# Self-attention of a Perceiver block: VectorE's sum of squares moved between the halves of the scores, the output scaled before the row sums, two copies of values moved from ScalarE

## The chip, the core and the metric

The kernel runs on one core of a Trainium2 chip. The core has five engines that run side by side, each with its own queue of instructions that it takes in order: TensorE (PE in the profile; its weight loads are the row PEld), VectorE (DVE), ScalarE (ACT), GpSimd (POOL) and SyncE (SP), which here only issues DMAs. An instruction that needs the result of another engine waits for a semaphore, and everything behind it on its own engine waits too. The metric is the time of one execution on the device in microseconds, less being better.

## What is computed

A block of three layers over x, 16 sequences of 64 latents with 512 features, each layer adding to x: a cross attention to a context of 512 tokens for each sequence, a differential self attention among the 64 latents, and a feed-forward network whose inputs and weights are rounded to FP4 blocks of 16. Each layer starts with a layer norm without weights. The change touches only the self attention:

```
q, k = rope(x @ Wq.T), rope(x @ Wk.T)        # 8 heads, each of two halves of 32
v    = x @ Wv.T                              # 8 heads of 64
w1   = softmax(q1 @ k1.T * 32**-0.25)
w2   = softmax(q2 @ k2.T * 32**-0.25)
o    = (w1 - lam * w2) @ v
ms   = mean(o * o, axis=-1)                  # for each row and head
o    = (o * rsqrt(ms + eps) * ln_w + ln_b) * (1 - LAMBDA_INIT)
x    = x + o @ Wo.T
```

## The kernel before, in words

The 1024 rows of x are eight tiles x0 to x7 of 128 rows, two sequences each. Products with weights run as three matmul groups: data and weights are split into a high and a low part, and high x high, high x low and low x high are added in PSUM (`terms`, L121, three groups of four matmuls for a 128x512 output).

The program has four parts: the preparation of the latents, the cross attention over 16 sequences (with the quantising of the feed-forward weights in between), the self attention, and the feed-forward network. Self attention overlaps with its neighbours: tiles 0 and 1 are started inside the last part of the cross attention (end of `cross_attention`), tiles 2 to 7 are the loop of `SelfAttention.rest`, and the last steps of tiles 6 and 7 lie among the first matmuls of the feed-forward network.

The steps for one tile t, and their engines, are:

- `product` (PE, L121): Wq, Wk and Wv of the tile; `rope` (DVE L1218 and L1220, then an addition on POOL, L1226) makes rc_q and rc_k.
- `values` (ACT, L1201): four copies of 64x256 that take the values out of PSUM, two (h) for each sequence e of the tile.
- `turn_qk` (PE L171, ACT L1236): transposes qt and kt, copied to qT and kT; `turn` does the same for the next tile's normalised input (zt, then zh on ACT and zl on DVE, L129 and L130); `turn_w` for the attention weights (wt, wT).
- `scores` (PE L1248): 64 small matmuls into two PSUM tiles, sc_0 and sc_1, one for each half of the heads' pairs.
- `softmax` (DVE): for each half a maximum (L1265, mx) and a subtraction (L1266, ex). `exp` (ACT L1275) then takes both halves in one instruction.
- `sum` (DVE L1280 to L1283): the row sums, their reciprocal, and the factor of lambda. `mix` multiplies by them (DVE L1288) and adds the two softmaxes on POOL (L1291, tile w).
- `weigh` (PE L1316): attention weights times values, output o in two PSUM tiles. `squares` (ACT L1327) squares it into SBUF, `rms` sums the squares (DVE L1332, ms) and has POOL make the reciprocal root (`rstd`: L136, then a power at L137). `scale` (DVE L1338, two instructions) multiplies o by it.
- `turn_o` (PE L171, tile ot): transposes the scaled output; ACT applies ln_w and ln_b (L1348) and makes the high part (L129), POOL the low part (L130, ol). `out` (PE): the product with Wo, tile wo; DVE adds it to x (L1368).

In one pass n of the loop these steps belong to three tiles: the products of tile n, the mixing of tile n-1 and the output of tile n-2; `end(n)` at the close of the pass holds the scores and softmax of tile n together with weigh, squares and rms of tile n-1. `end` is also called for tiles 0 and 1.

The order on each engine is the order in which the program records its instructions, fixed by `in_order`, which ties each instruction of an engine to the one before it. Some preparing steps of the feed-forward network are placed among them. DVE's order for tile n within `end` and the next pass is: mx, ex (first half), mx, ex (second half), ms of tile n-1, the row sums of tile n, and then, in the next pass, `scale` of tile n-1, `mix` of tile n, `rope` of tile n+1. POOL's order is: the power for tile n-1, w of tile n, ol of tile n-1, rc_q and rc_k of tile n+1. On PE the transposes ot of tile n-1 stand between Wk and Wv of tile n+1.

PSUM has three tiles of one bank for products and transposes (`ps_mm`), which are handed round: a matmul that writes one waits until the last reader of its previous content is done.

Of the kernel before, what the change touches and what calls it, by code (L numbers as in the profile page):

```python
# [9 lines left out]
F32 = mybir.dt.float32  # L10
# [9 lines left out]
P = 128  # L20
# [3 lines left out]
S = 64  # L24
N = 512
NJ = N // P
NT = B * S // P
# [427 lines left out]
def _latents(ctx, tc, cm, sc, i, cw, cx, sa):  # L455
# [261 lines left out]
    for g, _ in enumerate(groups):  # L717
        heads(g, "k", w_k, sc.k, 1.0)
        heads(g, "q", w_q, sc.q, S**-0.5, cw.bq)
        if g + 1 < len(groups):  # L720
            for p in groups[g + 1]:
                turn(p)
                upper(p)
                lower(p)
        values(g)
# [3 lines left out]
def cross_attention(tc, cm, sc, i, cw, cx, w1, w2, att, quant):  # L729
# [263 lines left out]
    for b in range(B):  # L993
# [38 lines left out]
        if last:  # L1032
            att.split("Wq", 2)
        scores(b, 0)
        softmax(b, 0)
        around(b + 1, 2, 3)
        keys(b, 3)
        cx.fetch(b + 2, 1)
        cx.low(b + 1, 2)
        cx.high(b + 1, 3)  # L1040
        tick()
        values(b, 0)
        cx.every(b + 1)
        cx.low(b + 1, 3)
# [5 lines left out]
        if b == 0:  # L1050
            load_o(0)
            load_o(1)
        values(b, 1)
        begin(b + 1)
        cx.fetch(b + 2, 2)
# [6 lines left out]
        turn(b, 0, 1)  # L1062
        scores(b, 1)
        softmax(b, 1)
        around(b + 2, 0, 1)
        if done is not None:
# [67 lines left out]
class SelfAttention:  # L1134
# [60 lines left out]
    def values(self, t):  # L1195

        v = self.st["v", t] = self.w1.tile([P, 2, KC, S], F32, tag="v", bufs=4, name=f"v_{t}")
        ps = self.st.pop(("ps", t, "Wv")).rearrange("p (c h d) -> p c h d", h=2, d=S)
        for e in range(2):
            for h in range(2):  # L1200
                self.nc.scalar.copy(v[h * S : (h + 1) * S, e], ps[e * S : (e + 1) * S, :, h, :])  # L1201

    def rope(self, t, name):
        nc, w1, sa = self.nc, self.w1, self.sa
# [48 lines left out]
                        stop=True,  # L1253
                    )

    def softmax(self, t):

        nc = self.nc
        mx = self.cm.small.tile([P, 16], F32, tag="mx", name=f"mx_{t}")
        ex = self.st["ex", t] = self.w1.tile([P, 16, S], F32, tag="q_hl", name=f"ex_{t}")  # L1260
        for n, ps in enumerate(self.st.pop(("sc", t))):
            half = slice(8 * n, 8 * n + 8)
            sc = ps[:, :, : KC * S].rearrange("p s (c t) -> p s c t", t=S)
            m = mx[:, half].rearrange("p (s c) -> p s c", s=2)
            nc.vector.tensor_reduce(m, sc, AX.X, ALU.max)  # L1265
            nc.vector.tensor_tensor(  # L1266
                ex[:, half, :].rearrange("p (s c) t -> p s c t", s=2),
                sc,
                m.unsqueeze(3).to_broadcast([P, 2, KC, S]),
                ALU.subtract,  # L1270
            )
# [97 lines left out]

    def end(self, n, sum=True):  # L1370

        if n < NT:
            self.turn_qk(n)
        if 0 <= n - 1:
            self.turn_w(n - 1)
        if n + 1 < NT:
            self.turn(n + 1)
        if n < NT:
            self.scores(n)
        if 0 <= n - 1:  # L1380
            self.weigh(n - 1)
            self.squares(n - 1)
        if n < NT:
            self.softmax(n)
            self.exp(n)
        if 0 <= n - 1:
            self.rms(n - 1)
        if n < NT and sum:
            self.sum(n)

    def rest(self, ff, last):

        first, second = (ff.norm_steps(t) for t in range(2))
        norms = iter(first[:2] + second[:1] + first[2:4] + second[1:2] + first[4:] + second[2:])


        parts = {3: (1, 0, 1), 4: (1, 2, 1), 5: (1, 2, 0), 6: (0, 2, 0), 7: (1, 2, 0)}  # L1400

        def steps(n, part):
            for _ in range(parts[n][part] if n in parts else 0):
                next(norms)()

        for n in range(2, NT):
            self.product(n, "Wq")
            self.scale(n - 2)
            self.product(n, "Wk")
            if n == NT - 1:  # L1410
                ff.weights(("g", 1))
            self.mix(n - 1)
            self.turn_o(n - 2)
            self.rope(n, "Wq")
            self.product(n, "Wv")
            if n == NT - 1:
                ff.weights(("u", 1), ("d", 0))
            self.values(n)
            if n + 1 < NT:
                self.norm(n + 1)  # L1420
            self.rope(n, "Wk")
            steps(n, 0)
            if n == NT - 1:
                ff.turn(0)
            self.out(n - 2)
            last.get(n, lambda: None)()
            if n == 2:
                ff.weights(("g", 0), ("u", 0))
            steps(n, 1)
            self.end(n)  # L1430
            steps(n, 2)
        assert not list(norms)
        ff.gate((0, 0))
        self.scale(NT - 2)
        self.mix(NT - 1)
        ff.up((0, 0))
        ff.gated((0, 0))
        self.turn_o(NT - 2)
        ff.turn(1)
        ff.gate((0, 1))  # L1440
        self.turn_w(NT - 1)
        ff.quantise((0, 0))
        ff.weights(("d", 1))
        ff.gate((1, 0))
        self.weigh(NT - 1)
        self.squares(NT - 1)
        self.rms(NT - 1)
        self.out(NT - 2)
        ff.weights(("g", 2))
        ff.up((0, 1))  # L1450
        self.scale(NT - 1)
        ff.hidden((0, 1))
        self.turn_o(NT - 1)
        ff.up((1, 0))
        ff.hidden((1, 0))
        ff.turn_h((0, 0))
        self.out(NT - 1)
        ff.weights(("u", 2), ("d", 2))
        self.cm.in_order()
# [271 lines left out]
```

## Time and profile before

| what | value |
|---|---|
| runs | 911.80, 912.67 and 987.52 us, median 912.67 us |
| the profiled execution | 912.59 us, span of the core 910.7 us |
| busy DVE, ACT, POOL in the span | 682.1, 399.9, 330.5 us |
| TensorE clock granted | 1.0 |
| from 576 to 731 us: tiles 0 to 7 of the self attention | 155 us, of which PE is busy 147.06 |
| before 576 us and after 731 us | PE busy 564.58 of 576.0, and 175.26 of 180.0 |

The profile is of one execution of 912.59 us; the span from its first to its last instruction is 1.9 us shorter. Two of the three runs and the profiled execution lie within 0.9 us of each other. A line of the timeline gives start, duration, engine, line of the code, operation, output and inputs with their sizes, the number of instructions merged, and in brackets the idle time of the engine just before, with the instruction that ended it. In what follows a time "at 645.06" is counted from the start of the span.

### The profile page before, as it was taken

To read this page: it belongs to the slowest core of one execution; us is meant where nothing else is said; L and a number is where in the kernel's file an instruction comes from. 1 tells how busy PE (TensorE), PEld (TensorE's weight loads), DVE (VectorE), ACT (ScalarE), POOL (GpSimd) and SP (SyncE) were. 2 spreads that over 40 slices of the span, in tenths; PEclk is the share of its full clock that TensorE was granted. 3 is DMA by queue.
4 is the path that set the end of the run, shared out by engine and by line. 5 is a ranking of instruction groups with operands and counts; after the bars stand their busy time and mean duration, and the time that the engine had idled before them with its cause. 6 is when DMAs were issued, how large, how long until landed. Compare 5 with 4: busy or idle time off the path is not lost.

```text
span 910.7 us, 17129 instructions
## 1 busy us (share of the span) xinstructions
PE 886.9 (97%) x6550; PEld 733.2 (81%) x6550; DVE 682.1 (75%) x1394; ACT 399.9 (44%) x782; POOL 330.5 (36%) x376
## 2 busy tenths in 40 slices
PE   5999999999999999999999999999999999999998
PEld 5898777878787887888778877778777788888886
DVE  7545467878799787786997964586878797888875
ACT  4464344544545444445444545545454423322221
POOL 5255153326254353263443621547564330100000
PEclk9999999999999999999999999999999999999999
DMA  7464565554555445345544452140005530000000
GB/s 241 176 242 138 152 187 166 152 178 146 150 161 150 159 157 174 112 138 151 161 147 144 133 149 102 47 185 2 2 1 212 229 139 12 12 12 12 13 13 24
DMA packets 80235, 111.11 MB, mean 122 GB/s; under 512 B 33161, under 2 KB 38809, under 8 KB 78873
## 3 DMA queue, kind: packets, MB, share of 16 engines
q1 hardware_dynamic: 79992, 109.48, 37.5%
q8 instruction: 52, 0.85, 0.4%
q0 software_dynamic: 160, 0.52, 0.2%
q14 instruction: 31, 0.25, 0.1%
HBM read 84.26 MB, written 25.72 MB: 121 GB/s over the span
## 4 chain that ended last, share of the span: by engine, by line
PE 85%; DVE 7%; ACT 3%; DMA 2%; issue 1%; SPq 1%; POOL 1%; ACTq 0%; DVEq 0%; POOLq 0%
PE pk L121 18%; PE pv L121 18%; PE gu L121 13%; PE dn L121 7%; PE av L904 4%; PE sim L836 4%; PE prt L171 3%; PE po L121 3%; PE Wv L121 2%; PE lv L121 2%; PE wo L121 2%; PE lq L121 2%; PE lk L121 2%; DVE ex L1266 1%; PE ht L171 1%; DMA raw_wo<-in_w_out_dram 1%
## 5 line engine op out<-in xcount | busy, mean ns | idle before, releaser
L121 PE MATMUL pv<-xvh,x 128*128 128x512 f32 x512 | 133.1, 392 | 0.0
L121 PE MATMUL pk<-x,xkh 128*128 128x512 f32 x512 | 130.5, 397 | 0.3 <-DVE k L810 0.3
L121 PEld LDWEIGHTS pk<-x,xkh 128*128 128x128 f32 x512 | 93.7, 188 | 26.0 <-issue 4.0
L121 PEld LDWEIGHTS pv<-xvh,x 128*128 128x128 f32 x512 | 95.3, 188 | 23.3 <-issue 2.2
L810 DVE TENSOR_TENSOR k<-pk,row 128x512 f32<-128x512 f32 x64 | 43.6, 683 | 47.0 <-PE pk L121 46.8
L823 ACT ACTIVATE v<-pv,rs 128x512 f32<-128x512 f32 x64 | 43.9, 686 | 79.4 <-PE pv L121 79.3
L859 ACT ACTIVATE pr<-pr,least 128x576 f32<-128x576 f32 x64 | 49.2, 772 | 55.1 <-DVE least L855 54.8
L368 POOL TENSOR_TENSOR x<-raw,x 128x512 fp32r<-128x512 f32 x32 | 44.2, 1382 | 78.0 <-ACT x L362 71.6
L121 PE MATMUL pk<-x,xkl 128*128 128x512 f32 x256 | 68.7, 390 | 0.0
L121 PE MATMUL pv<-xvl,x 128*128 128x512 f32 x256 | 68.5, 389 | 0.0
L121 PE MATMUL gu<-uT,fx 128*128 128x512 f32 (+1 forms) x288 | 67.8, 378 | 0.0
L121 PE MATMUL gu<-gT,fx 128*128 128x512 f32 (+1 forms) x288 | 65.5, 375 | 0.0
L121 PEld LDWEIGHTS gu<-gT,fx 128*128 128x128 f32 x288 | 52.3, 188 | 7.6
L121 PEld LDWEIGHTS gu<-uT,fx 128*128 128x128 f32 x288 | 51.9, 188 | 7.2
L121 PEld LDWEIGHTS pk<-x,xkl 128*128 128x128 f32 x256 | 48.1, 188 | 10.4
L121 PEld LDWEIGHTS pv<-xvl,x 128*128 128x128 f32 x256 | 48.1, 188 | 10.2
L855 DVE CUSTOM_DVE_ANT_0 pr<-sim,mask 128x576 f32<-128x576 f32 x64 | 45.9, 754 | 6.2 <-PE sim L836 5.3
L321 DVE BATCH_NORM_STATS2 cst<-nat 128x6 f32<-128x512 f32 x64 | 42.8, 669 | 3.6 <-DMA nat<-in_ctx_dram 3.6
L121 PE MATMUL dn<-dT,hh 128*128 128x512 f32 x176 | 44.7, 393 | 0.6 <-ACT hh L129 0.6
L205 ACT ACTIVATE qe_h<-qe_h,mmagic 128x512 f32<-128x512 f32 (+1 forms) x24 | 16.5, 687 | 64.3 <-DVE qe_h L202 64.3
L871 ACT COPY prT<-prt 128x512 f32<-128x512 f32 x64 | 34.1, 585 | 18.1 <-PE prt L171 18.1
L904 PEld LDWEIGHTS av<-v,prT 128*64 128x64 f32 x1024 | 36.7, 138 | 5.6 <-issue 5.6
(302 smaller groups left out, 1963.0 us busy)
## 6 DMA issues: line engine op xcount, KB each, us to landing
nat<-in_ctx_dram SPq DMA_DIRECT2D x16, 1024.0 KB
raw<-in_ctxT_dram SPq DMA_DIRECT2D x64, 256.0 KB
d_d<-qhl_d SPq DMA_DIRECT2D x11, 512.0 KB
row<-rs_d SPq DMA_DIRECT2D x16, 256.0 KB
g_d<-qhl_g SPq DMA_DIRECT2D x8, 512.0 KB
u_d<-qhl_u SPq DMA_DIRECT2D x8, 512.0 KB
gT<-g_d SPq DMA_DIRECT2D x4, 1024.0 KB
uT<-u_d SPq DMA_DIRECT2D x4, 1024.0 KB
```

What stands on the lines that cost most here:

```text
L121: self.nc.tensor.matmul(ps, lhsT=p[i], rhs=p[j], start=start and n == 0, stop=stop and n == last)
L171: self.nc.tensor.transpose(pt[:, c * P : (c + 1) * P], src[:, c * P : (c + 1) * P], self.ident)
L205: nc.scalar.activation(e, e, AF.Relu, bias=self.mmagic, scale=MAGIC)
L321: nc.vector.bn_stats(st, self.nat[b][:, j, :])
L368: by.tensor_tensor(lo, self.raw[:, c, :], f32(hi), ALU.subtract)
L810: nc.vector.tensor_tensor(k[:, S : S + N], ps, cx.row[b], ALU.mult)
L823: nc.scalar.mul(v, ps, cx.rs[b][:, t : t + 1])
L836: nc.tensor.matmul(pss[r][c * S : (c + 1) * S, h, :half], lhsT=queries[b % 2][rows, m, :], rhs=st["k"][m][rows, at : at + half], start=Tru ...
L855: nc.vector.tensor_tensor_reduce(two(pr), ps[:, :, :half], two(mask), -1.0, BIG, ALU.add, ALU.min, least)
L859: nc.scalar.activation(pr, pr, AF.Exp, bias=least, scale=-1.0, accum_out=st["tot"][:, t : t + 1])
L871: nc.scalar.copy(prT, pt.rearrange("p (j q) -> p j q", q=P))
L904: nc.tensor.matmul(st["av"][rows, 2 * a + r, :], lhsT=w[:, rows], rhs=v[:, at : at + S], start=(n == 0), stop=(n == len(pairs) - 1),)
```

## The change

Three things move; no arithmetic of the result is changed.

1. `softmax` takes the halves that it is to do, so that `end` can call it once for each half. `rms` of the tile before (the sum of squares on DVE and the two POOL instructions behind it) now stands between the halves.
2. `scale` of the tile before moves from the next pass, after the product Wq, into `end`: after `exp` and ahead of `sum`.
3. In `values`, for tile 0 alone, the two copies of the second sequence go to DVE.

```
     def values(self, t):
 ...
         for e in range(2):
+            copy = self.nc.vector.tensor_copy if t == 0 and e else self.nc.scalar.copy
             for h in range(2):
-                self.nc.scalar.copy(v[h * S : (h + 1) * S, e], ps[e * S : (e + 1) * S, :, h, :])
+                copy(v[h * S : (h + 1) * S, e], ps[e * S : (e + 1) * S, :, h, :])

-    def softmax(self, t):
+    def softmax(self, t, ns=range(2)):
 ...
     def end(self, n, sum=True):
-        if n < NT:
-            self.turn_qk(n)
-        if 0 <= n - 1:
+        self.turn_qk(n)
+        if n:
             self.turn_w(n - 1)
         if n + 1 < NT:
             self.turn(n + 1)
-        if n < NT:
-            self.scores(n)
-        if 0 <= n - 1:
+        self.scores(n)
+        if n:
             self.weigh(n - 1)
             self.squares(n - 1)
-        if n < NT:
-            self.softmax(n)
-            self.exp(n)
-        if 0 <= n - 1:
+        self.softmax(n, range(1))
+        if n:
             self.rms(n - 1)
-        if n < NT and sum:
+        self.softmax(n, range(1, 2))
+        self.exp(n)
+        if n:
+            self.scale(n - 1)
+        if sum:
             self.sum(n)

     def rest(self, ff, last):
 ...
             self.product(n, "Wq")
-            self.scale(n - 2)
             self.product(n, "Wk")
 ...
         ff.gate((0, 0))
-        self.scale(NT - 2)
         self.mix(NT - 1)
```

DVE's order becomes: mx, ex of the first half of tile n, ms of tile n-1, mx, ex of the second half, the two instructions of `scale` for tile n-1, the row sums of tile n, `mix` of tile n, `rope` of tile n+1. DVE has two instructions more and ACT two fewer, all for tile 0. The orders of PE, POOL and SP do not change. On ACT one step of the feed-forward network (the normalising fz of its tile 2, L166, in the pass of tile 7) comes two instructions later. In the changed program the two copies on DVE wait for the two on ACT, and the transposes zt of tile 1 take the PSUM tile of qt and wait for the copy qT, where they took that of the values before and waited for the four copies; the product Wq of tile 1 now takes the values' tile and waits for DVE's copies.

More of the change, by code (lines that the diff above doesn't have):

```diff
@@ L1254, in scores @@
                     )
-    def softmax(self, t):
+    def softmax(self, t, ns=range(2)):
         nc = self.nc
-        mx = self.cm.small.tile([P, 16], F32, tag="mx", name=f"mx_{t}")
-        ex = self.st["ex", t] = self.w1.tile([P, 16, S], F32, tag="q_hl", name=f"ex_{t}")
-        for n, ps in enumerate(self.st.pop(("sc", t))):
+        if ns[0] == 0:
+            self.st["mx", t] = self.cm.small.tile([P, 16], F32, tag="mx", name=f"mx_{t}")
+            self.st["ex", t] = self.w1.tile([P, 16, S], F32, tag="q_hl", name=f"ex_{t}")
+        mx, ex = self.st["mx", t], self.st["ex", t]
+        for n in ns:
+            ps = self.st["sc", t][n]
             half = slice(8 * n, 8 * n + 8)
```

## The prediction

> **What bounds the kernel now.** First the page's list of engines: TensorE is busy nearly throughout, so only a time in which it stands still can be won, and its clock is granted in full.
>
> ```profile
> PE 886.9 (97%) x6550; PEld 733.2 (81%) x6550; DVE 682.1 (75%) x1394; ACT 399.9 (44%) x782; POOL 330.5 (36%) x376
> ```
>
> Then TensorE's waits from 575 to 760 us, each row a waiting operation, its releaser, us in total, times and the longest:
>
> ```profile
> PE ot L171 <- DVE on L1338: 6.1, 7, 1.5
> PE zt L171 <- ACT v L1201: 0.8, 1, 0.8
> ```
>
> These two are what the change aims at: seven waits of the output's transposes for the scaling, and the wait for the copies of values. The first row counts from the modelled end of the matmul before. By starts it is more: a group of four matmuls follows the next at 0.91 us, so ot could start 0.91 after the last group of Wk. It starts 1.63 late for tile 0, 0.90, 0.89, 0.90, 0.87 and 0.90 for tiles 1 to 5, and 1.17 for tile 6: 7.26 us.
>
> Whether it can be won shows in the timeline of one pass, TensorE first (ot of tile 2, then the transposes of tile 4):
>
> ```profile
> 643.26 1.07 PE L121 MATMUL Wk<-Wkh,zl 128*128 128x512 f32 x4
> 645.06 0.65 PE L171 MATMUL ot<-ident,on 128*128 128x128 f32 x4 [0.73 <-DVE on L1338]
> 651.45 0.60 PE L171 MATMUL kt<-ident,rc_k 128*128 128x128 f32 x4
> ```
>
> VectorE in the same pass:
>
> ```profile
> 638.59 0.68 DVE L1265 TENSOR_REDUCE mx<-sc 128x8 f32<-128x512 f32 x1
> 639.38 0.69 DVE L1266 TENSOR_TENSOR ex<-sc,mx 128x512 f32<-128x512 f32 x1
> ...
> 641.31 0.67 DVE L1332 TENSOR_REDUCE ms<-on 128x8 f32<-128x512 f32 x1
> 642.57 1.22 DVE L1280 TENSOR_REDUCE sm<-ex 128x16 f32<-128x1024 f32 x1 [0.59 <-ACT ex L1275]
> ...
> 644.25 0.75 DVE L1338 TENSOR_TENSOR on<-o,rstd_o 128x256 f32<-128x256 f32 x2
> 644.92 1.21 DVE L1288 TENSOR_TENSOR ex<-ex,sm 128x1024 f32<-128x1024 f32 x1
> ```
>
> And GpSimd:
>
> ```profile
> 642.34 1.66 POOL L137 TENSOR_TENSOR rstd_o<-rstd_o,mhalf 128x8 f32<-128x8 f32 x1
> 646.28 1.31 POOL L1291 TENSOR_TENSOR w<-ex 128x512 f32<-128x512 f32 x1 [2.28 <-DVE ex L1288]
> 647.54 1.30 POOL L130 TENSOR_TENSOR ol<-oT,oh 128x512 fp32r<-128x512 f32 x1
> 648.80 1.29 POOL L1226 TENSOR_TENSOR rc_q<-rc_q,rs_q 128x512 f32<-128x512 f32 x1
> 650.05 1.28 POOL L1226 TENSOR_TENSOR rc_k<-rc_k,rs_k 128x512 f32<-128x512 f32 x1
> ```
>
> The reader is to see a second chain. GpSimd does w as soon as mix (644.92) is over, then ol, rc_q and rc_k without a gap, and rc_k ends at 651.33; TensorE's kt, which needs it, starts at 651.45. One pass later kt does wait, in the weight loads:
>
> ```profile
> 667.33 0.42 PEld L171 LDWEIGHTS kt<-ident,rc_k 128*128 128x128 f32 x4 [0.18 <-POOL rc_k L1226]
> ```
>
> There rc_k ended at 667.27, so kt follows it by 0.06, and the slack at 651.45 was 0.06 us. From kt it goes on to the copies, the scores, mx 2.89 later, mix, GpSimd and the next kt: a loop of 2.89 + 6.33 + 1.36 + 3.77 + 1.28 + 0.06 = 15.69 us (kt to mx, mx to mix, mix to w, w to rc_k, its length, the release) beside a pass of 15.75. **The loop over GpSimd is as long as the pass with its stall.** A stall taken from ot must come back at kt unless mix comes earlier.
>
> **The change, part by part: the pass.** I count from mx of the first half (before, 638.59 = 0). Before: ex 0.79, mx 1.39, ex 2.11, ms 2.72, exp on ScalarE 2.89 (641.48), row sums 3.98, scale 5.66, mix 6.33.
>
> After: ex 0.79, ms 1.39. Its squares are there: ScalarE ended them at 639.36 = 0.77. The second mx is 0.61 later, 2.00; its ex 0.72 on, 2.72; exp 0.78 on, 3.50; the sums could start 1.09 after that, 4.59. GpSimd starts 0.75 after ms, as before (641.31, 642.06), at 2.14; the power starts 0.28 later and takes 1.65, until 4.07; VectorE, idle from 3.41, scales at 4.12. Behind this new wait stand the row sums, mix and rope. Scaling takes 0.67 to its successor, so the sums start at 4.79, not 4.59; then 1.26 to the reciprocal, 0.29 to the lambda factor, 0.26 to mix: **mix at 6.60, which is 0.27 later than before**. The scaled output is 1.54 earlier: ot could start at 4.12 + 0.81 = 4.93, that is 7.8 after kt, while TensorE reaches it 8.47 after kt (635.70 to 644.17). The wait for scaling goes.
>
> What is late next is kt. With qt transposed earlier, its copy no longer delays kT on ScalarE, some 0.04 less from kt to mx. The loop becomes 15.69 + 0.27 - 0.04 = 15.92, against 15.75 of the pass now: **0.17 longer for each pass**, with TensorE waiting about 1 us at qt and kt instead of 0.9 at ot. The product with the low part of the output doesn't add to it: ol ends 13.4 after kt, TensorE asks for it at 13.5.
>
> **The copies of tile 0.** Before: four copies at 587.90 in 1.50 us, qT at 589.42, kT at 589.91, zt at 589.45, the scores at 590.55, Wq of tile 1 at 591.39. After: two copies until 588.65, qT at 588.67, kT at 589.16, zt after qT at 589.30, the scores after kT (ends 589.75) at 589.80, zh at 590.04 and done at 590.64, Wq at 590.68. Gain **0.71**. VectorE's copies start behind ScalarE's at 588.70. No such copy is in the trace. The nearest row, VectorE's own 64x256 reading of PSUM (o from av, two in 0.88), gives an end at 589.58. [...] A gain beyond 0.75 is excluded, as ScalarE's queue loses no more.
>
> **From tile 1 to the end.** Before, kt of tiles 1 to 7: 602.85, 619.94, 635.70, 651.45, 667.33, 683.13, 699.38.
>
> - Tile 1: TensorE 0.71 earlier would be 602.14, rc_k allows 602.19. mx of tile 1, before at 607.12, comes at 606.41.
> - Tile 2: rc_k allowed 619.84; now 619.84 - 0.71 + 0.28 = 619.41. The 1.63 of tile 0's ot is gone, but only 0.53 is left of 0.71 + 1.63.
> - Tiles 3 and 4: 15.92 each, 635.33 and 651.25, leads of 0.37 and 0.20.
> - Tile 5: GpSimd's additions took 0.18 longer there (rc_q 1.47, beside VectorE's L202); 16.10 gives 667.35. Tile 6: 683.27. Tile 7, with the same 0.18: 699.37. The lead is gone.
> - The end is different. wt of tile 6 waited 0.30 for VectorE's fx, which comes earlier now, and kt of tile 7 had 0.37 to spare that is used up above. The scores start at about 700.8 (before 700.87), the feed-forward products at 702.3, and ot of tile 6 follows them at 707.87 without its 1.17: before 709.08, **lead 1.2**. mx of tile 7 comes at 701.8 (before 702.63), its mix at 708.4, w ends at 711.1, and wt, asked for at 711.5, doesn't wait.
>
> From there TensorE has hardly a wait (its rows until the end show 0.6, dn for hh), and weights loaded after ot's successors shift with them. **Sum: 1.2 us**, from 912.59 of the profiled execution to 911.4; the median of the runs, 912.67, is the same within 0.1.
>
> **The rivals.**
>
> 1. *The stall is really won.* If GpSimd's additions came earlier than my loop allows, all of 7.26 + 0.71 would go: 912.6 - 8.0 = 904.6. For it: the wait at ot is the largest row. Against: w needs mix, mix the sums, and no row shortens that. Chance 0.1.
> 2. *The scaling's wait for GpSimd holds the pass (slower).* In the loop VectorE stands idle before scaling; whatever makes the root later delays sums, mix, w, rc_k and kt one for one. Place: L136 and L137 in tiles 2 to 7. The point: each 0.1 costs 0.5 over five loops, so from 0.24 us it eats the 1.2. For it: GpSimd has other work just before (in tile 4 L199 until 655.25, in tile 5 until 671.89), and 1.65 us for a power of eight numbers is mostly fixed cost that I can't take apart. Against: by the sums above it is free at least 0.4 us before ms is ready. Half a us later: 911.4 + 2.5 = 913.9. Chance 0.2.
> 3. *The copies don't do what they are for.* VectorE's copies wait for ScalarE's, so if zt or Wq hung on them for longer, 0.71 would go at the front; part of it is lost in the loop anyway, and the end gives some 0.7: 911.9. Chance 0.1.
>
> **The numbers.** Forecast 0.6, at 911.4; its own range, with 0.1 of error in each of six loops and 0.5 between executions, 910.3 to 912.6. For 8 in 10 I leave out the first rival and reach down to 909.2 for a loop 0.3 shorter, and up to 914.0 for the second. 2% is 18 us, about what a measurement can tell from no change; all that stands still here is 8 us, so faster by 2% has 0.01, slower 0.01, the same 0.98.
>
> **What would show it.** In the profile after: the row of ot waiting for scaling gone or under 0.5; a new row of kt (and qt) waiting for rc_k and rc_q on GpSimd, some 5 to 6 us; VectorE idle 0.7 before L1338, released by the power; mix some 6.6 after mx; passes of 15.9; Wq of tile 1 at 590.7. I am wrong if kt doesn't wait (mix came earlier than I have it, or GpSimd is faster) or if the passes exceed 16.1 (GpSimd's root late).

## The result and the profile after

The changed kernel takes 911.05 us (median of its runs) beside 912.28 us for the kernel before: ratio 0.9987, 95% interval 0.9981 to 0.9994. That is 1.2 us less. By the interval it stands clear of no change, but it is far inside the 2% that were called no change; the forecast was 911.4. One of the twenty executions of each kernel was slow, 987.52 us before and 1478.24 us after (there at a granted clock of 0.559), and the ratio is without these two. The profiled span went from 910.7 to 909.4 us.

The list of engines in the page of the changed kernel; each entry is busy us, share of the span and instructions:

```profile
PE 888.6 (98%) x6550; PEld 733.5 (81%) x6550; DVE 684.8 (75%) x1396; ACT 399.7 (44%) x780; POOL 330.8 (36%) x376
```

TensorE's waits in the changed kernel from 575 to 760 us (us in total, times, longest):

```profile
PE kt L171 <- POOL rc_k L1227: 3.4, 6, 0.6
PE zt L171 <- ACT qT L1237: 0.6, 1, 0.6
PE wo L121 <- POOL ol L130: 0.4, 1, 0.4
PE wt L171 <- ACT qT L1237: 0.2, 1, 0.2
PE sc L1249 <- ACT kT L1237: 0.2, 1, 0.2
PE qt L171 <- POOL rc_q L1227: 0.2, 1, 0.2
```

The row of ot waiting for the scaling, 6.1 us before, is gone. Six waits of kt for GpSimd's rc_k have come instead. So the stall was not won; it has moved along the pass. Where to, the timeline of TensorE in the same pass as before (ot of tile 2, kt of tile 4) shows:

```profile
642.89 1.07 PE L121 MATMUL Wk<-Wkh,zl 128*128 128x512 f32 x4
643.80 0.60 PE L171 MATMUL ot<-ident,on 128*128 128x128 f32 x4
...
648.82 1.10 PE L121 MATMUL wo<-Woh,ol 128*128 128x512 f32 x4
649.98 0.66 PE L171 MATMUL qt<-ident,rc_q 128*128 128x128 f32 x4
651.21 0.66 PE L171 MATMUL kt<-ident,rc_k 128*128 128x128 f32 x4 [0.57 <-POOL rc_k L1227]
```

ot follows the last group of Wk by 0.91 us, the normal distance of two groups: no wait. But qt starts 1.16 after the last group of wo instead of 0.91, and kt 1.23 after qt instead of 0.43: 1.05 us in this pass, against 0.89 that ot lost before. VectorE of the changed kernel in that pass:

```profile
638.15 0.68 DVE L1269 TENSOR_REDUCE mx<-sc 128x8 f32<-128x512 f32 x1
...
639.54 0.68 DVE L1336 TENSOR_REDUCE ms<-on 128x8 f32<-128x512 f32 x1
...
642.28 0.76 DVE L1342 TENSOR_TENSOR on<-o,rstd_o 128x256 f32<-128x256 f32 x2 [0.73 <-POOL rstd_o L137]
642.95 1.21 DVE L1284 TENSOR_REDUCE sm<-ex 128x16 f32<-128x1024 f32 x1
...
644.75 1.22 DVE L1292 TENSOR_TENSOR ex<-ex,sm 128x1024 f32<-128x1024 f32 x1
```

Counted from mx, the scaling starts at 4.13, the row sums at 4.80 and mix (the last line) at 6.60; VectorE idles 0.73 in front of the scaling. GpSimd of the changed kernel:

```profile
646.11 1.29 POOL L1295 TENSOR_TENSOR w<-ex 128x512 f32<-128x512 f32 x1 [3.87 <-DVE ex L1292]
647.36 1.31 POOL L130 TENSOR_TENSOR ol<-oT,oh 128x512 fp32r<-128x512 f32 x1
648.62 1.30 POOL L1227 TENSOR_TENSOR rc_q<-rc_q,rs_q 128x512 f32<-128x512 f32 x1
649.87 1.28 POOL L1227 TENSOR_TENSOR rc_k<-rc_k,rs_k 128x512 f32<-128x512 f32 x1
```

w starts 1.36 after mix, the next three follow without a gap, rc_k ends at 651.15 and kt starts 0.06 later. The loop over GpSimd is 2.89 + 6.60 + 1.36 + 3.76 + 1.28 + 0.06 = 15.95 us, and the pass, kt of tile 3 to kt of tile 4 (635.26 to 651.21), is 15.95. No wait at ot is left, so this loop sets the pace alone.

For what follows I divide the self attention by starts of TensorE's transposes. Runs differ by up to 1.6 us in when tile 0 reaches its kt, which comes from work ahead of the change, so all is counted from there. A stretch is the time from one such start to another. In us, from one profile of each kernel:

| kernel | kt of tile 0 to kt of 1 | kt of 1 to kt of 7 | kt of 7 to wt of 7 | wt of 7 to ot of 7 | sum |
|---|---|---|---|---|---|
| before | 14.77 | 96.53 | 13.39 | 9.49 | 134.18 |
| after | 14.11 | 97.37 | 11.99 | 9.51 | 132.98 |
| difference | -0.66 | +0.84 | -1.40 | +0.02 | -1.20 |

The six passes cost 0.84, the front and the end give more back. The sum is the 1.2 us of the measured medians.

### The profile page after: what moved, and what is told of

Same layout as the page of the kernel before. It is cut to its first block, busy times and chain, and to the rows that moved or that the text cites. A ratio compares the mean times of both kernels' runs of the same rounds, so it can differ in the third digit from the quotient of the medians.

```text
span 909.4 us, 17126 instructions
## 1 busy us (share of the span) xinstructions
PE 888.6 (98%) x6550; PEld 733.5 (81%) x6550; DVE 684.8 (75%) x1396; ACT 399.7 (44%) x780; POOL 330.8 (36%) x376
## 4 chain that ended last, share of the span: by engine, by line
PE 83%; DVE 7%; POOL 5%; DMA 2%; ACT 2%; issue 1%; SPq 0%; DVEq 0%; POOLq 0%; ACTq 0%
PE pk L121 18%; PE pv L121 18%; PE gu L121 13%; PE dn L121 7%; PE av L904 4%; PE sim L836 4%; PE prt L171 3%; PE po L121 3%; PE lv L121 2%; PE lq L121 2%; PE lk L121 2%; POOL rstd_o L137 1%; PE ht L171 1%; DMA raw_wo<-in_w_out_dram 1%; POOL rc_q L1227 1%
```

## The experiments

The theory on trial is the loop over GpSimd: a pass is as long as the way from kt over scores, softmax, mix and GpSimd's four additions to the next kt. The rivals are that the stall at ot was the limit, and that the gain has another source than the edits it is put down to. A ratio below is the recorded one; it can differ from the quotient of the two medians beside it, by up to 0.0006.

**The copies alone.** The kernel before, with part 3 of the change only:

```
         for e in range(2):
+            copy = self.nc.vector.tensor_copy if t == 0 and e else self.nc.scalar.copy
             for h in range(2):
-                self.nc.scalar.copy(v[...], ps[...])
+                copy(v[...], ps[...])
```

> The kernel before with the third part alone: VectorE takes two of tile 0's four copies. Loop theory (a pass of the self attention is as long as the loop kt, scores, mix, GpSimd's additions, kt): everything behind tile 0 shifts by 0.7 us and the passes stay at 15.75, so kt of tile 7 at 698.7 and 0.7 us less than before, a ratio of 0.9992. Rival (the loop swallows the front's gain, and the change's 1.2 us come from the reordering): less than 0.3 us gained.

Measured 911.08 us beside 912.29, ratio 0.9983 (0.9976 to 0.9990). These two copies by themselves bring what the whole change brings, and 0.5 more than expected. By the stretches: 14.09, 96.57, 12.67, 9.51, sum 132.84. The front gives 0.68, as forecast. The surprise is the third: 0.72 between kt and wt of tile 7, 110 us after the copies. ScalarE there, in the kernel before:

```profile
697.48 0.82 ACT L166 ACTIVATE fz<-x,mv_f 128x512 f32<-128x512 f32 x1
698.20 0.71 ACT L205 ACTIVATE qe_x<-qe_x,mmagic 128x512 f32<-128x512 f32 x1
698.92 0.59 ACT L129 CAST fx<-xt 128x512 fp32r<-128x512 f32 x1
```

And ScalarE with the copies alone:

```profile
696.71 0.72 ACT L205 ACTIVATE qe_x<-qe_x,mmagic 128x512 f32<-128x512 f32 x1
697.46 0.59 ACT L129 CAST fx<-xt 128x512 fp32r<-128x512 f32 x1
697.94 0.81 ACT L166 ACTIVATE fz<-x,mv_f 128x512 f32<-128x512 f32 x1
```

The normalising of feed-forward tile 2 (fz), which is not read before 734.36 in the kernel before, stands ahead of fx in the one and behind it in the other. fz of tile 2 is recorded after the program has fixed its order (`in_order`), so it lies outside it, the scheduler places it, and the whole change has the second order too. What the exchange holds up is VectorE, which makes the low part of fx behind ScalarE's cast. Here are this low part and the first mx of tile 7 in the kernel before:

```profile
699.54 0.69 DVE L130 TENSOR_TENSOR fx<-xt,fx 128x512 fp32r<-128x512 f32 x1 [2.98 <-ACT fx L129]
...
702.63 0.66 DVE L1265 TENSOR_REDUCE mx<-sc 128x8 f32<-128x512 f32 x1
```

And with the copies alone:

```profile
698.08 0.69 DVE L130 TENSOR_TENSOR fx<-xt,fx 128x512 fp32r<-128x512 f32 x1 [2.27 <-ACT fx L129]
...
701.17 0.66 DVE L1266 TENSOR_REDUCE mx<-sc 128x8 f32<-128x512 f32 x1
```

Five more of VectorE's instructions stand between the two, and in both kernels mx starts 3.09 after the low part. The scores are over at 701.78 and 700.88, before mx starts, so it is VectorE's queue that holds mx. Counted from kt of tile 7, the low part starts at 0.16 before and at -0.56 here: these are the 0.72.

**fz moved alone.** The kernel before, with an ordering without a semaphore that holds fz of tile 2 behind the cast fx of tile 0. All other engines keep their order, and no copy of values moves:

```
-            cm.shifted(z, cm.x[t], st.pop(("mv", t)))
+            made = cm.shifted(z, cm.x[t], st.pop(("mv", t)))
+            if t == 2:
+                self.behind(made, self.cast)
```

> The kernel before with one edit on ScalarE alone: the scaling of tile 2 for the feed-forward (fz, L166 in the kernel before) is held behind the cast of tile 0's transposed input (fx), where the copies' edit had put it too; no copy of values moves. If that exchange is the second half of what the copies gained: fx ends 0.72 us sooner, the first row maximum of tile 7 starts 2.5 us after its kt instead of 3.25, tile 6's output is transposed 9.0 after that kt instead of 9.7, and the time is 911.6 beside 912.3 (ratio 0.9992). If the end's gain comes from the copies themselves: 912.3, ratio 1.000. kt of tiles 1 to 7 as in the kernel before under either.

Measured 911.41 beside 912.26, ratio 0.9994 (0.9986 to 1.0002). The interval just includes no change, so the time alone doesn't show it; the trace does. TensorE's transposes of tile 6's output, in the kernel before (kt of tile 7 at 699.38):

```profile
709.08 0.66 PE L171 MATMUL ot<-ident,on 128*128 128x128 f32 x4 [1.01 <-DVE on L1338]
```

And with fz moved (kt of tile 7 at 699.31):

```profile
708.32 0.66 PE L171 MATMUL ot<-ident,on 128*128 128x128 f32 x4 [0.48 <-DVE on L1338]
```

9.70 after kt before, 9.01 here. The stretches are 14.79, 96.51, 12.70, 9.51, sum 133.51: only the third differs from before, by 0.69. The copies alone gave 1.34, of which 0.68 at the front and 0.72 at the end; with 0.67 for fz alone, the copies proper are worth 0.67.

**The whole change with fz put back.** fx and fz change places on ScalarE, and nothing else (fz is recorded ahead of the cast, its preparing steps are left out of the written order and stay where they were):

```
         cm.transpose_chunks(pt, self.st.pop(("z", t)), KC)
+        if t == 0:
+            self.third = self.norm_steps(2)
+            self.third[0]()
+            self.third[1]()
```

> The whole change, with fz put back ahead of fx on ScalarE, and nothing else moved. If the exchange is needed for the gain at the end: the first maximum of tile 7 starts 0.8 us later after its kt, the weights' transpose waits 0.3 for the low part of fx, and w of tile 7 ends at some 711.9 where it is asked for at 711.7, so 0.3 to 0.8 is lost: 911.65, ratio 0.9994. If the earlier scaling alone gives the end's gain: 911.05, ratio 0.9987. kt of tiles 1 to 7 as with the whole change.

Measured 911.15 beside 912.26, ratio 0.9990 (0.9983 to 0.9997). By the time it stands nearer to the second case, and the intervals with and without fz overlap too far to tell a difference of 0.1 to 0.4. The trace is clearer: stretches 14.13, 97.34, 12.39, 9.54, sum 133.40, so 0.40 of the 1.40 at the end go, the first mx of tile 7 comes 0.50 later after its kt, and a wait appears (these lines are numbered 4 higher in this kernel):

```profile
PE wt L175 <- POOL w L1299: 0.2, 1, 0.2
```

The other 1.00 stays: that part comes from the new order on VectorE. It shows at ot of tile 6, which comes 8.40 after kt of tile 7, as in the whole change (8.38) and not as before (9.70). In this order of VectorE fz decides only when w of tile 7 is ready. Both cases were too simple; the two causes overlap.

**The order without the copies.** The change without part 3.

> The kernel after without the copies: the squares' sum between the halves and the scaling ahead of the sums, all four copies on ScalarE. Loop theory: passes of 15.92 in place of 15.75, ot no longer waits, kt of tile 7 at about 700.1 (before 699.38), and the end of the self attention gives back 1.2 of it, so ot of tile 6 at 708.5 (before 709.08): 0.5 us less than before, ratio 0.9994; with the copies alone it adds up to the 1.2 of the whole change. Rival (waits at ot are really won): 7 us less.

Measured 911.75 beside 912.29, ratio 0.9994 (0.9987 to 1.0000). The median is as expected, but the interval reaches no change, so here too the stretches decide: 14.77, 97.33, 12.01, 9.51, sum 133.62. That is the front as before, the passes as in the whole change, the end as in the whole change (fz stands behind fx here as well). That the copies alone (-1.34) and the order alone (-0.56) don't add up to -1.20 is the end, which each takes and which can be taken once.

**Each half of the order alone.** First the squares' sum between the halves, with the scaling left in the next pass:

```
-        if n < NT:
-            self.softmax(n)
-            self.exp(n)
-        if 0 <= n - 1:
-            self.rms(n - 1)
+        self.softmax(n, range(1))
+        if n:
+            self.rms(n - 1)
+        self.softmax(n, range(1, 2))
+        self.exp(n)
```

> The kernel before with the first part alone: the squares' sum between the halves, scaling behind the sums as before. Loop theory: the second half, exp, sums, scaling and mix all come 0.61 later, nothing is gained by the earlier root since scaling stands behind the sums; passes of 16.34 (the loop over ot) for 15.75, 4 us more: 916.5, ratio 1.0046. Rival (each part gains by itself): at or under the time before.

Measured 917.87 beside 912.29, ratio 1.0055 (1.0041 to 1.0068): slower by 5.6, where some 4 were expected (916.5). The profile is of the fastest of the four executions, 916.67 us, and its stretches sum to 138.38, 4.20 more than before. The other 1.4 is in no trace; two of the other executions, 918.19 and 918.2 us, show a granted clock of 0.997, where the profiled one has 0.999.

Then the scaling ahead of the row sums, with the squares' sum left behind both halves:

```
         self.softmax(n)
         self.exp(n)
-        if 0 <= n - 1:
+        if n:
             self.rms(n - 1)
-        if n < NT and sum:
+            self.scale(n - 1)
+        if sum:
             self.sum(n)
```

> The kernel before with the second part alone: scaling ahead of the sums, the squares' sum behind both halves as before. Loop theory: VectorE waits for GpSimd's root until 5.45 after the first maximum, so mix comes at 7.93 in place of 6.33 and the pass is 17.25, TensorE waiting 2.3 at kt: 8.2 us more, 920.5, ratio 1.009. Rival (each part gains by itself): at or under the time before.

Measured 920.3 beside 912.29, ratio 1.0084 (1.0071 to 1.0098): slower by 8.0. VectorE of the kernel with the scaling alone shows why:

```profile
641.43 0.68 DVE L1268 TENSOR_REDUCE mx<-sc 128x8 f32<-128x512 f32 x1
...
646.87 0.76 DVE L1341 TENSOR_TENSOR on<-o,rstd_o 128x256 f32<-128x256 f32 x2 [2.05 <-POOL rstd_o L137]
...
649.34 1.22 DVE L1291 TENSOR_TENSOR ex<-ex,sm 128x1024 f32<-128x1024 f32 x1
```

The scaling idles VectorE for 2.05 us while GpSimd makes the root, the sums stand behind it, and mix starts 7.91 after mx instead of 6.33: 1.58 later, and the pass is 17.25, 1.50 longer. With the squares alone it is 6.93 and 16.35, 0.60 and 0.60. In both, the pass grows with the delay of mix, almost one for one. But with the squares alone it is not GpSimd that holds TensorE. No row there has kt waiting for rc_k, and the wait at ot is longer than before:

```profile
PE ot L171 <- DVE on L1341: 10.3, 7, 2.1
```

Scaling, still behind the sums, comes as much later as mix does; the loop over GpSimd works out to 15.69 + 0.60 = 16.29, which stays 0.06 below the pass. With the scaling alone kt waits for rc_k in six passes. Each half is a loss; the first shortens the wait that the second makes.

**One addition taken out of GpSimd's row.** The whole change, with ol of tiles 0 to 5 made on VectorE between the two ropes (`low_o`, not shown, holds the subtraction):

```
-            self.turn_o(n - 2)
+            self.turn_o(n - 2, low=False)
             self.rope(n, "Wq")
+            self.low_o(n - 2, self.nc.vector)
```

> The kernel after with the output's low part (tile ol, tiles 0 to 5) computed by VectorE between the two ropes and no longer by GpSimd between w and rc_q. Loop theory: one of four additions leaves GpSimd's part of the loop, rc_k then waits for VectorE's rope at 13.8 after kt, the pass is 15.17 for 15.93, kt waits 0.3, and the time is 906.4, ratio to before 0.9935. Rival (a pass is as long as VectorE's work in it, which grows by 0.6): the passes are 16.5, 3.7 us more than the kernel after, 914.8.

Measured 908.82 beside 912.23, ratio 0.9961 (0.9946 to 0.9976). It beats both kernels, which shows that GpSimd's row is in the loop. The pass is 15.38 where 15.17 were expected. VectorE in this kernel, between the two ropes:

```profile
646.16 0.81 DVE L1369 TENSOR_TENSOR ol<-oT,oh 128x512 fp32r<-128x512 f32 x1
646.89 0.68 DVE L1219 TENSOR_TENSOR rc_k<-Wk,cos 128x512 f32<-128x512 f32 x1
```

GpSimd of the same kernel at the same time:

```profile
646.38 1.75 POOL L1227 TENSOR_TENSOR rc_q<-rc_q,rs_q 128x512 f32<-128x512 f32 x1
648.31 1.28 POOL L1227 TENSOR_TENSOR rc_k<-rc_k,rs_k 128x512 f32<-128x512 f32 x1 [0.18 <-DVE rs_k L1221]
```

rc_q takes 1.75 us instead of 1.30 while VectorE's ol runs beside it, and rc_k then waits 0.18 for VectorE, whose rope comes later. Of the 1.25 that leave GpSimd's row, 0.68 come back: from rc_q to rc_k it is 1.93 instead of 1.25. 1.25 - 0.68 = 0.57, and 15.95 - 0.57 is the measured 15.38. The time is 2.4 above the expected 906.4: 0.21 in each of six passes is 1.3, and from kt to wt of tile 7 it takes 12.91 instead of 11.99, which is 0.9.

**The same move in the kernel before.** The same edit.

> The same move of the low part in the kernel before. Loop theory: there the loop over scaling and ot sets the pass at 15.75 and GpSimd's loop is only just as long, so nothing is gained: within 0.3 us of before, ot still waits 0.9 in each pass. Rival (GpSimd's additions set the pass already before): 15.2 for a pass and about 4 us less. Rival (VectorE's work sets it): 3.7 us more.

Measured 912.15 beside 912.23, ratio 0.9998 (0.9990 to 1.0007); the pass stays at 15.75:

```profile
PE ot L171 <- DVE on L1338: 6.2, 7, 1.5
```

That row is TensorE's largest wait there, as it was, and no row has kt waiting for rc_k. The scaling is a second limit, and no shorter than the loop, so shortening the first brings nothing. With the reordering the second limit is gone and the first can be shortened: this is what the change is good for, and it doesn't collect it itself.

**A shorter root.** The whole change, where ScalarE's squares are scaled by 1/64 as they are made, and GpSimd takes the power alone (the small constant under the root is left out):

```
-            self.nc.scalar.activation(by_half(o)[:, h], po, AF.Square)
+            self.nc.scalar.activation(by_half(o)[:, h], po, AF.Square, scale=S**-0.5)
...
-        self.st["r", t] = cm.rstd(ms, 8, RMS_EPS, 1.0 / S, f"o_{t}")
+        r = self.st["r", t] = cm.small.tile([P, 8], F32, tag="rstd8", name=f"rstd_o_{t}")
+        self.nc.gpsimd.tensor_tensor(r, ms, cm.mhalf, ALU.pow)
```

> The kernel after with one GpSimd instruction less in the root: the squares are scaled by 1/8 on ScalarE so that their sum is the mean, and the small constant under the root is left out, so only the power remains. Loop theory: the root is ready 0.28 earlier, scaling no longer holds the sums, mix comes 0.2 earlier, the pass is 15.72 for 15.93, and the time is 909.9, ratio 0.9974. Rival (scaling's wait for the root costs nothing, since the sums wait for exp anyway): as the kernel after, 911.05.

Measured 910.11 beside 912.23, ratio 0.9976 (0.9966 to 0.9985). One short GpSimd instruction less, the scaling's wait falls from 0.73 to 0.45:

```profile
640.78 0.75 DVE L1343 TENSOR_TENSOR on<-o,rstd_o 128x256 f32<-128x256 f32 x2 [0.45 <-POOL rstd_o L1338]
641.52 1.22 DVE L1284 TENSOR_REDUCE sm<-ex 128x16 f32<-128x1024 f32 x1
```

mix stands 6.38 after mx, 0.22 earlier, the pass is 15.74, and the stretch of six passes 96.40 instead of 97.37. So 0.22 in front of mix is worth 0.97: it counts 4.4 times. Five of the six passes are 0.21 to 0.23 shorter. The one from kt of tile 5 is 0.10 longer: w starts there 1.67 after mix instead of 1.36, and why stays open.

**Both.** ol on VectorE, and the shorter root.

> The kernel after with both: the low part on VectorE between the ropes, and the shorter root without its small constant. Loop theory: passes of 14.97, TensorE's own work in a pass being 14.86: 905.2, ratio 0.992. Rival (VectorE's work sets the pass): 914 or more.

Measured 906.71 beside 912.23, ratio 0.9940 (0.9926 to 0.9953), passes of 15.17: 0.21 below those of ol alone, so the two add up, and they miss the expected 14.97 by the same 0.20 as there. The time misses the expected 905.2 by 1.5.

**ol on VectorE with fz behind fx.** The two edits shown above, together.

> The whole change with the product's low part of the output on VectorE for tiles 0 to 5 (as in e5_after_low), and fz held behind fx. There the weights' transposes waited 0.3 us for the low part of fx and 0.5 for w of tile 7. If both come from fz: the two waits go, and the time is 0.8 below that run's, 908.0 (ratio 0.9953). If not: 908.8.

Measured 908.24 beside 912.26, ratio 0.9960 (0.9947 to 0.9972). The time looks better than the 908.82 without fz, yet by the trace nothing is gained: 14.10, 93.78, 12.92, 9.52, sum 130.32, against 14.13, 93.76, 12.91, 9.57, 130.37. The difference lies ahead of the self attention (kt of tile 0 at 587.26 and 588.10), so I don't count it. ScalarE of this kernel shows why:

```profile
693.97 0.72 ACT L205 ACTIVATE qe_x<-qe_x,mmagic 128x512 f32<-128x512 f32 x1 [0.90 <-DVE qe_x L202]
694.72 0.59 ACT L1546 CAST fx<-xt 128x512 fp32r<-128x512 f32 x1
```

With ol in VectorE's queue its part of qe_x comes later, and ScalarE waits 0.90 for it, in the place where fz had stood. fz filled a gap there and delayed nobody. Of the two waits of wt, the one for fx stays at 0.28; the one for w falls from 0.51 to 0.19, but wt of tile 7 starts no earlier after kt (12.92 against 12.91).

## Why the prediction was right, and where not

**What bounds it: right.** kt waits for rc_k in six passes, the loop's terms add up to the pass, and three kernels with another length of the same loop (17.25, 15.74, 15.38) went where their terms put them, except for the 0.2 of rc_q in the last. The fourth (16.35, the squares alone) was held by the other loop, over scaling and ot, as was expected of it.

**The pass: right to 0.03.** Scaling at 4.12 and measured 4.13, sums 4.79 and 4.80, mix 6.60 and 6.60. The loop was put at 15.92 and is 15.95: the 0.04 taken off from kt to mx, for a qT copied sooner, did not come (635.26 to 638.15 is 2.89, as before). For the new waits at kt and qt 5 to 6 us were named; the rows show 3.4, 0.4 for wo and 0.2 for qt, while by starts the pass shown alone has 1.05. The rows count only from the modelled end of the last matmul, which the prediction had said of ot's row and then forgot for its own.

**The front: right.** 0.71 was put down for the copies, of which rc_k of tile 1 was to let through 0.66; 0.66 to 0.68 were measured. VectorE's two copies, in the changed kernel, with what waits behind them:

```profile
588.55 0.87 DVE L1202 COPY v<-Wv 64x256 f32<-64x256 f32 x2 [0.97 <-ACT v L1202]
...
590.54 0.69 DVE L130 TENSOR_TENSOR zl<-zt,zh 128x512 fp32r<-128x512 f32 x1 [0.19 <-ACT zh L129]
```

0.87 for two, against 0.88 in the row that the forecast took from the trace before (o from av). zl waits 0.19 for ScalarE, so the copies hold nobody.

**From tile 1 on: right.** kt of tiles 2 to 7 at 619.41, 635.33, 651.25, 667.35, 683.27, 699.37 by the forecast; 619.29, 635.26, 651.21, 667.35, 683.29, 699.43 measured. This profile reaches kt of tile 0 0.13 sooner than the one before, so the agreement flatters a little: from kt of tile 1 to kt of 7 it is 97.37 against 97.18 by the forecast, and from there to ot of tile 6 8.38 against 8.50. Two small misses nearly cancel.

**The end: right in its time, wrong in one source.** ot of tile 6 was put at 707.87 and started at 707.81; wt of tile 7 doesn't wait, as forecast. The lead of ot is the new order's, as forecast: it stays with fz put back. But the step "VectorE's fx, which comes earlier now" was put down without its cause and without a price. It rests on fz changing places with fx, which the section on the change names and the sum never prices. With fz put back, wt of tile 7 does wait, and 0.40 of the end's 1.40 are lost in the trace. What was off is therefore the term for the copies. They were given 0.71 at the front, most of it lost in the passes, a gain beyond 0.75 was excluded, and the third rival priced their failure at 0.5 (911.9 against 911.4). As an edit they bring 1.34 by the stretches and 1.2 by the medians, because the scheduler moved fz along with them. In the whole change the trace divides the 1.20 so: the copies at the front 0.66, fz 0.42, and for the new order of squares and scaling, the main edit, 0.12 are left (in the kernel with fz put back, 0.81 lost in six passes and 1.00 won between kt and wt of tile 7). Single profiles bear 0.1 of such a division and not much less, and the times by themselves don't tell these parts from one another.

**The rivals.** That the stall is really won, 904.6: refuted, it came back at kt. That the root holds the pass: its slope was right (0.22 counted 4.4 times, five were named), and the point from which it decides was not reached; the idle time in front of the scaling is 0.73 as foreseen. What spoke for it, that the power's 1.65 us is mostly fixed cost, does not hold: the same power on 128x1 took 0.55 to 0.56 in the self attention of both kernels (L149), so 1.1 of the 1.65 come with the other seven columns. That the copies fail: refuted.

**The range.** 0.6 and 0.5 on top of 911.4 make 912.5, not 912.6. And 18 us is not what a measurement can tell from no change: the interval here is 1.2 us wide.

## What to carry to other kernels

Before a stall is attacked, follow the next queue round to the same place and add up its loop: if that is as long as the pass, the stall comes back one wait later, and here the two halves of an edit cost 5.6 and 8.0 us one by one, and together they gained 0.5 by the medians, which the interval does not tell from nothing. In a diff of orders, price each instruction that moves, also one that the diff's author never touched: a filler of 0.8 us that changed places was worth 0.4 to 0.7 us by the traces, as much as the edit. Once the second limit is out of the way, take work out of the loop that is left: one addition moved off GpSimd gave 2.2 us after the change (911.05 to 908.82) and nothing before it.

## What the runs showed of the hardware

A GpSimd addition of 128x512 (rc_q) took 1.75 us instead of 1.30 when a VectorE instruction with two SBUF inputs (ol, 0.81 us) had started some 0.22 us before it. It took 1.74 to 1.76 in each of the four passes from 638 us on in three of the kernels in which VectorE makes ol: the move after the change, the same move before it, and the move with fz behind fx. Beside VectorE's rope instructions, which read PSUM and SBUF, w and ol on GpSimd took 1.29 and 1.31 in the changed kernel. The lengthening of 0.45 is less than the 0.59 for which ol still ran. No run here took the overlap away while all else stayed, so it is not shown that the overlap is the cause. Two inputs in SBUF are not the only case: beside L202 on VectorE, which has one (0.54 us), the same addition took 1.47 in the kernel before (rc_q at 664.55).
